# Moving PSUM banks, query buffers and the order of keys and values around a cross-attention stage, with each batch's first two heads split by rows

## The chip, the cores and the metric

The kernel runs on one core of a Trainium2 chip, in one launch. The metric is device time in microseconds (us), measured for the whole launch; the figure is the median of several runs. The engines are named as in the profile: PE (matmul), PEld (weight load, which overlaps PE), DVE (VectorE), ACT (ScalarE), POOL (GpSimd), SP (the engine that issues DMAs). Each runs its own list of instructions in order, and waits for others by semaphores.

## The reference

Four batches of 512 rows with 512 features go through four blocks, each added to the residual `x` with a gate (the tanh of a given number). Cut to what matters:

```python
# 1: selective scan over the context (512 rows x 256), gated by the normed x
x = x + tanh(g_xattn[0]) * ssm(ctx, layernorm(x), ...)        # 16 states per channel
# 2: ternary FFN: activations rounded to 8 bits, weights to -1, 0, 1
x = x + tanh(g_ffn[0]) * out(silu(gate(xn)) * val(xn))        # hidden 2048
# 3: cross attention, 16 heads of 128
q = rmsnorm((xn @ Wq).reshape(B, Sq, H, D), gq)
k = rmsnorm((ctx @ Wk).reshape(B, Skv, H, D), gk)
v = (ctx @ Wv).reshape(B, Skv, H, D)
attn = softmax(einsum('bqhd,bkhd->bhqk', q, k) * scale)
x = x + tanh(g_xattn[1]) * (einsum('bhqk,bkhd->bqhd', attn, v).reshape(B, Sq, H * D) @ Wo)
# 4: four experts, row r goes to expert r % 4
x = x + tanh(g_ffn[1]) * (silu(gate) * up) @ down
```

## The kernel before

**Work and its stages.** Products in fp16 are made of high and low halves: `split` (L238) writes both halves of a tile from PSUM or SBUF, the high half on ACT (L240), the low half on DVE (L241), and `mm3` (L243) makes three matmuls per pair (L249). The stages, per batch b:

- `front(b)` (L487) prepares the scan's inputs from context and x; `scan(b)` (L569) runs the recurrence, with most of its work on DVE (L622) and POOL (L183), and exps on ACT (L615).
- `bitnet(b)` (L670) is the ternary FFN. It ends with four updates of x, one per block of 128 rows (L755).
- `attention(b)` (L779) returns generators that the main loop steps through: `keys` (L799, per group of four heads: pk, ksq, kT), `values` (L850), `queries` (L865: weights wq by DMA, twelve matmuls into pq, high and low half qT, the squares sq), `query_norms` (L882: psq, ssq, and rqs on POOL), `scores` (L898: ps, and its row maxima nmx on DVE), `softmax` (L907: exps pr on ACT, normed high and low halves hl, and a transposing DMA to pT), `weight` (L952: pav), `weighted_sum` (L961: oT), `project` (L966, per four heads: pwo, added to x). `prepare(t)` norms one block of 128 rows and transposes it into axnT.
- `early_experts` (L1098) runs the experts of batches 0 to 2, `last_experts` (L1124) those of batch 3, behind its attention.

**The prologue** (L1162 to L1223) uses pools that close at its end: `pro` in SBUF and `psp`, four PSUM banks. It runs front and scan of batch 0; makes the ternary weights (`ternary`, tiles w8 with the tag "v", of VB buffers, stored to DRAM); runs the ternary FFN of batch 0, with `prepare` behind each row block; then `first_values` (L338), which computes batch 0's values from all four groups' weights, into tiles ov (tag "v" as well, VB buffers), and stores them in DRAM; then the weights of the attention's first groups, the keys of group 0, and the contexts of batches 2 and 3. When these pools have closed, `psa` opens (L1224): four PSUM banks, two with the tag "m" for pq, pk, pw, psq, pav and pwo, two with the tag "s" for ps. With it opens `at` in SBUF (L1226), which holds v, wq, qT, pr, hl, pT, oT and wo. Another four PSUM banks, `pss`, exist from the outset and serve front, scan, the ternary FFN and the experts. `ak` is an SBUF pool that exists from the outset, with axnT, sq, the keys and their weights.

**The main loop** (L1256 to L1297) runs over units i = (batch, head). At unit i it takes the query phase of unit i+2, the score phase of i+1 and the weighting phase of i, interleaved in ten slots. Between the slots it feeds the scan and FFN of the next batch: `rate` grows by RATE_S (0.5) or RATE_B (0.8) per slot, and a step is taken for each whole; LEADS says how many units ahead of a batch its scan begins. At the slots KPOS (5 and 9) a piece of the next group's keys is made. Other work, the staging of weights and the early experts, is filled in behind softmax's exps.

A scheduler (Tile) adds the semaphores to this order; each engine runs its own part of the program in order. When a tile takes a buffer or bank, it waits until the last use of the one before is over.

Of the kernel before, what the change touches and what calls it, by code (L numbers as in the profile page):

```python
# [30 lines left out]
F16 = mybir.dt.float16  # L31
# [9 lines left out]
P = 128  # L41
B = 4
L = 512
# [49 lines left out]
PT = 3  # L93
MT = 0
AV = 4
VB = 2
WB = 5
ATAG = {"ps": "s"}
ABUF = {"m": 2, "s": 2}
LO_POOL = {(b, h, 1) for b in range(3) for h in range(9, 16)}  # L100
HL = 2
PRE = 1
LEADS = {1: 16, 2: 17, 3: 17}
SZR = 12
NEXT = 2
LEAD_B = 6

# [2 lines left out]
def flamingo_kernel(  # L110
# [20 lines left out]
    def psum(pool, name, tag="m", bufs=None):  # L131
        if tag == "a":
            role = name.rstrip("_0123456789")
            tag = ATAG.get(role, "m")
            bufs = ABUF[tag]
        kw = {} if bufs is None else {"bufs": bufs}
        return pool.tile([P, 512], F32, tag=tag, name=name, **kw)
# [100 lines left out]
    def split(w, hi, lo, S):  # L238

        nc.scalar.activation(hi, w, AF.Copy, scale=S)  # L240
        nc.vector.scalar_tensor_tensor(lo, w, S, hi, ALU.mult, ALU.subtract)  # L241
# [537 lines left out]
    def attention(b):  # L779
# [13 lines left out]
                "q" if b else "t",  # L793
            )

        kns, vals, kqs, probs = [None] * NG, [None] * NG, [None] * NH, [None] * NH
        scs, nmxs = [None] * T, [None] * 2

        def keys(hg, ps_tile=ap):  # L799
# [62 lines left out]
                nc.sync.dma_start(wv.rearrange("p s k c -> p (s k c)"), wv_d[hg])  # L862
                vals[hg] = list(values_of(b, hg, wv, ap, v_tile))

        def queries(i):  # L865
            hg, h = divmod(i, HG)
            hn = f"{b}{hg}{h}"
            wq = at.tile([P, 2, T, HD], F16, tag="wq", name=f"wq{hn}", bufs=WQ)
            nc.sync.dma_start(wq.rearrange("p s k c -> p (s k c)"), wq_d[hg][:, h * 1024 : (h + 1) * 1024])

            ps = ap(f"pq{hn}")
            xnT = xnTs[0]
            mm3(ps, [(wq[:, 0, k], wq[:, 1, k], xnT[:, 0, k], xnT[:, 1, k]) for k in range(T)])
            sq = ak.tile([P, L], F32, tag="sq", name=f"sq{hn}", bufs=2)
            qT = at.tile([P, 2, L], F16, tag="qT", name=f"qT{hn}", bufs=2)
            split(ps, qT[:, 0], qT[:, 1], gqs)
            nc.scalar.activation(sq, ps, AF.Square, scale=QS)
            kqs[i] = [kns[hg][h // 2][:, :, :, h % 2], qT, sq]  # L880

        def query_norms(i):  # L882
            hg, h = divmod(i, HG)
            hn = f"{b}{hg}{h}"
            sq = kqs[i][2]
            ps = ap(f"psq{hn}")
            for c in range(T):
                nc.tensor.matmul(  # L888
                    ps[:, c : c + 1], sq[:, c * P : (c + 1) * P], ones[:, 0:1],
                    start=True, stop=True,  # L890
                )
            ssq = sm(T, "ssq", f"ssq{hn}")
            nc.scalar.activation(ssq, ps[:, 0:T], AF.Identity, bias=ceq[hg], scale=gfac)  # L893
            rqs = sm(T, "rqs", f"rqs{hn}")
            rsqrt(rqs, ssq)
            kqs[i][2] = rqs

        def scores(i, c):  # L898
            kT, qT, _ = kqs[i]
            rows = slice(c * P, (c + 1) * P)  # L900
            ps = ap(f"ps{b}{i}_{c}")
            mm3(ps, [(qT[:, 0, rows], qT[:, 1, rows], kT[:, :, 0], kT[:, :, 1])])
            nmx = nmxs[i % 2]
            nc.vector.tensor_reduce(nmx[:, c : c + 1], ps, AX.X, ALU.max, negate=True)  # L904
            scs[c] = ps

        def softmax(i, c0):  # L907

            rqs = kqs[i][2]
            hn = f"{b}{i}_{c0}"  # L910
            two = slice(c0, c0 + 2)
            nmx = nmxs[i % 2]
# [34 lines left out]
            nc.sync.dma_start_transpose(  # L947
                pT.rearrange("p c s k r -> p (c s k) r"), hl.rearrange("p c s k -> p (c s k)")
            )
            probs[i].append(pT)  # L950

        def weight(i, half, ps):  # L952
            hg, h = divmod(i, HG)
            cols = slice(h * HD, (h + 1) * HD)
            pT = probs[i][half]
            mm3(
                ps[:, half * 256 : (half + 1) * 256],
                [(v[:, 0, cols], v[:, 1, cols], pT[:, :, 0, k], pT[:, :, 1, k]) for k, v in enumerate(vals[hg])],
            )

        def weighted_sum(i, ps):  # L961
            o = at.tile([P, 2, L], F16, tag="oT", name=f"oT{b}{i}", bufs=4)
            split(ps, o[:, 0], o[:, 1], 1.0 / PS)
            return o

        def project(hg, os):  # L966
            nm = f"{b}{hg}"
# [12 lines left out]
                xr = xt[:, t, :]  # L980
                nc.vector.scalar_tensor_tensor(xr, ps, fo, xr, ALU.mult, ALU.add)

        os = []

        def step(i, phase):

            hg, h = divmod(i, HG)
            if phase == 0:  # L990
                if h == 0:
                    if i == 0 and b > 0:
                        for t in range(T):
                            prepare(t)
                    if KL == 0 and kns[hg] is None:
                        run(keys(hg))
                    if b < PRE:
                        values(hg)
                yield
                queries(i)  # L1000
                yield
                query_norms(i)
            elif phase == 1:
                probs[i] = []
                nmxs[i % 2] = sm(T, "nmx", f"nmx{b}{i}")
                scores(i, 0)
                yield
                scores(i, 1)
                softmax(i, 0)
                yield  # L1010
                scores(i, 2)
                yield
                scores(i, 3)
                softmax(i, 2)
            else:
                if h == 0 and b >= PRE:
                    values(hg)
                ps = ap(f"pav{b}{i}")
                for half in range(2):
                    weight(i, half, ps)  # L1020
                    yield
                os.append(weighted_sum(i, ps))
                if h == HG - 1:
                    project(hg, os)
                    os.clear()

        return step, keys, prepare

# [130 lines left out]
                    fill.pop(0)  # L1159

    ak = ctx.enter_context(tc.tile_pool(name="ak", bufs=1))
    with tc.tile_pool(name="pro", bufs=1) as pro, tc.tile_pool(name="psp", bufs=4, space=PSUM) as psp:  # L1162

        psv = pss

# [7 lines left out]
            wider["t"] = pro, MT  # L1173

        def iter_ps(name):
            return psum(psp, name, "mn"[int(name[-1]) % 2], 2)

        w3 = [
            ternary(pro, psv, [gate_wT[k * P : (k + 1) * P, :] for k in range(4)], [P, HID], 0, True),
# [24 lines left out]
        for name, bias in (("gate", gate_b), ("val", val_b)):  # L1204
# [4 lines left out]
        steps[0] = step  # L1209

        run(bitnet(
            0, wide, lambda name: psum(psp, name, "n", 2), biases, prepare, lambda name: psum(psp, name, "m", 2)
        ))


        def aside(name):
            return psum(pss, name)

        run(first_values(pro, aside))
        run(attention_weights(range(EARLY), pss))  # L1220
        run(keys(0, aside))
        for b in range(2, B):
            context(b, bigt, junk, psv, bigt)  # L1223
    psa = ctx.enter_context(tc.tile_pool(name="psa", bufs=4, space=PSUM))  # L1224
    at_pool = ctx.enter_context(ExitStack())
    at = at_pool.enter_context(tc.tile_pool(name="at", bufs=1))  # L1226

# [6 lines left out]
            estats[b][t] = row_stats(x_sb[b][:, t, :], f"e{b}{t}", XS, const.tile([P, 2], F32, name=f"est{b}{t}"))  # L1234

    in_bitnet = [False]
    behind, rate = [], 0.0

    def layer0(b):

# [11 lines left out]
            yield  # L1252


    n = B * NH
    for i in range(-2, n):  # L1256
        b2, h2 = divmod(i + 2, NH)
        for b4, lead in LEADS.items():
            if i + 2 + lead == b4 * NH:
                behind.append((b4, layer0(b4)))  # L1260
        while behind and behind[0][0] <= b2:
            run(behind.pop(0)[1])
        if KL == 0 and h2 == 0 and 0 < b2 < B:
            atts[b2] = attention(b2)
        if h2 == 0 and 0 < b2 < B:
            steps[b2] = atts[b2][0]
        if h2 == 0 and 0 < b2 < B:
            steps[b2] = atts[b2][0]
        q = steps[b2](h2, 0) if i + 2 < n else iter(())
        s = steps[(i + 1) // NH]((i + 1) % NH, 1) if 0 <= i + 1 < n else iter(())  # L1270
        w = steps[i // NH](i % NH, 2) if i >= 0 else iter(())
        for k, g in enumerate((q, s, q, s, w, s, w, s, w, q)):
            next(g, None)
            if behind:
                rate += RATE_B if in_bitnet[0] else RATE_S
                while rate >= 1 and behind:
                    rate -= 1
                    if next(behind[0][1], behind) is behind:
                        behind.pop(0)
            if k in KPOS:  # L1280
                j, c = divmod((i + 2) * len(KPOS) + KPOS.index(k) - KOFF, 4 * len(KPOS))
                j += 1
                b3, hg3 = divmod(j, NG)
                if c < 4 and 0 < j and b3 < B:
                    if c == 0 and hg3 == 0:
                        atts[b3] = attention(b3)
                    if c == 0:
                        keygen = atts[b3][1](hg3)
                    next(keygen)
                    if c == 3:  # L1290
                        next(keygen, None)
        if i == -2:
            fill.append(attention_weights(range(EARLY, NG), None))
        if i >= 0 and i % NH == NH - 1:
            finish(i // NH)
        if i == n - NH + STAGE_E:
            fill.append(early_experts())  # L1297
    while fill:
        filler(mark[0])
# [70 lines left out]
```

## Time and profile before

| what | us |
|---|---|
| runs shown | 2036.04, 2039.12, 2039.02 |
| median | 2039.02 |
| profiled execution | 2044.35 |
| its span | 2042.6 |
| mean granted TensorE clock | 0.874 |
| value tiles ov, first and last ACT instruction begin | 201.8 to 254.7 |
| last x update of the ternary FFN, batch 0 | 302.2 |
| first softmax exp | 338.4 |
| first scan of batch 1 | 367.7 |
| first softmax exp of batches 1, 2, 3 | 800.5, 1237.1, 1598.5 |
| last row block added by the attention of batch 3 | 2003.6 |

The table is one profiled execution but for the first two rows. The last row is followed by experts to the end of the span. A unit of attention takes some 23 to 29 us: 16 of them lie between the first exps of two batches. The profile's chain of work that ended last puts 19% of the span to PE, 7% to DVE, 5% to ACT, 5% to DMA; the rest of the page is read further down, where its lines are used. In a group's line, the form is out<-in with the program's names, then the count, the time, and what ended the idle time before it.

### The profile page before, as it was taken

The page shows a single profiled execution, that of the slowest core. Times are in us where ns is not written, and L with a number is a line of the kernel's source. Part 1 is how long each engine was busy: PE and PEld are TensorE (multiplying, and loading weights), DVE is VectorE, ACT ScalarE, POOL GpSimd, SP SyncE. Part 2 cuts the span into 40 slices and gives each one's busy share as a digit, 9 for nine tenths or more (in the row PEclk, how much of TensorE's full clock was granted, in tenths as well). Part 3 has the DMA queues.
Part 4 walks back from the last instruction along what each step waited for, and adds up shares of the span by engine and source line. Part 5 has one row for each costly group of instructions (what it writes and reads, how often), then busy time and mean ns, then how long its engine had stood idle before and what let it go on. Part 6 is the DMA issues. An engine that isn't in the chain of part 4 may idle for free. (4 is left out here: it accounts for less than half of the span.)

```text
span 2042.6 us, 27081 instructions
## 1 busy us (share of the span) xinstructions
PE 1608.2 (79%) x8238; PEld 903.3 (44%) x8238; DVE 1575.8 (77%) x2857; ACT 1320.4 (65%) x3118; POOL 1001.7 (49%) x926
## 2 busy tenths in 40 slices
PE   4465867667789877787989778778898879798988
PEld 1343322444444344454444444454444445445446
DVE  5898985999989787999887876999874555465654
ACT  5796566765758595565568663756476576757653
POOL 1884332876745378575436582765354240313211
PEclk8555987767899987899998988999999989899989
DMA  7554468789796877777658777688765775757854
GB/s 272 176 183 163 157 162 229 186 221 259 191 277 160 209 187 174 211 168 183 122 147 207 179 167 195 154 193 196 164 130 119 172 170 162 188 147 182 211 118 139
DMA packets 528242, 369.09 MB, mean 181 GB/s; under 512 B 425248, under 2 KB 427424, under 8 KB 521696
## 3 DMA queue, kind: packets, MB, share of 16 engines
q1 hardware_dynamic: 528096, 367.37, 71.0%
q8 instruction: 64, 1.05, 0.2%
q14 instruction: 82, 0.67, 0.1%
HBM read 220.22 MB, written 44.30 MB: 130 GB/s over the span
## 5 line engine op out<-in xcount | busy, mean ns | idle before, releaser
L183 POOL TENSOR_TENSOR h<-u,bc 128x512 f32<-128x512 f32 x256 | 339.3, 1346 | 84.6 <-PE py L590 49.1
L590 PE MATMUL py<-ident,h 128*128 128x128 f32 x1024 | 199.1, 339 | 135.9 <-DVE h L623 110.4
L615 ACT ACTIVATE dA<-delta,A 128x512 f32<-128x512 f32 x256 | 172.2, 685 | 137.0 <-DVE h L623 110.2
L622 DVE TENSOR_TENSOR_SCAN dA<-dA,h 128x512 f32<-128x512 f32 x200 | 240.8, 1217 | 20.1 <-POOL h L183 15.5
L249 PE MATMUL pav<-pT,v 128*128 128x256 f16 x1536 | 210.7, 294 | 47.9 <-DMA pT<-hl 19.9
L590 PEld LDWEIGHTS py<-ident,h 128*128 128x128 f32 x1024 | 164.1, 213 | 180.8 <-DVE h L623 133.8
L249 PE MATMUL ps<-kT,qT 128*128 128x512 f16 x768 | 212.5, 397 | 37.6 <-ACT pr L924 34.4
L249 PE MATMUL pq<-axnT,wq 128*128 128x512 f16 x768 | 204.9, 423 | 36.2 <-DMA axnT<-xsa 11.2
L904 DVE TENSOR_REDUCE nmx<-ps 128x1 f32<-128x512 f32 x256 | 173.2, 680 | 73.1 <-PE ps L249 72.2
L945 DVE SCALAR_TENSOR_TENSOR hl<-pr,den,hl 128x512 f16<-128x512 f32 x214 | 191.4, 911 | 30.1 <-ACT hl L942 16.7
L924 ACT ACTIVATE pr<-ps,nmx,rqs 128x512 f32<-128x512 f32 x256 | 197.1, 772 | 17.6 <-DVE hl L945 13.8
L249 PEld LDWEIGHTS <-v 128*128 128x128 f16 x1536 | 160.3, 105 | 105.9 <-issue 50.4
L249 PE MATMUL pwo<-wo,oT 128*128 128x512 f16 x768 | 180.3, 386 | 6.4 <-DVE oT L241 3.1
L944 POOL TENSOR_SCALAR hl<-pr,den 128x512 f16<-128x512 f32 x86 | 61.8, 719 | 186.9 <-issue 82.8
L249 PEld LDWEIGHTS <-wq 128*128 128x128 f16 x768 | 82.6, 109 | 147.1 <-issue 68.3
L249 PEld LDWEIGHTS <-cT 128*128 128x128 f16 x768 | 80.7, 106 | 146.0 <-issue 75.8
L183 POOL TENSOR_TENSOR g<-g,gv 128x512 f32<-128x512 f32 x64 | 84.3, 1319 | 111.1 <-DVE gv L724 56.1
L180 POOL TENSOR_TENSOR rqs<-ssq,mhalf 128x4 f32<-128x4 f32 x64 | 68.6, 1072 | 138.9 <-ACT ssq L893 123.5
L623 DVE TENSOR_TENSOR h<-dA,cc 128x512 f32<-128x512 f32 x200 | 133.8, 678 | 2.6
L249 PEld LDWEIGHTS <-qT 128*128 128x128 f16 x768 | 78.2, 103 | 122.9 <-issue 57.2
L249 PE MATMUL pk<-wk,cT 128*128 128x512 f16 x384 | 109.9, 431 | 28.2 <-ACT ssq L893 14.3
L942 ACT ACTIVATE hl<-pr,den 128x512 f16<-128x512 f32 x128 | 92.1, 719 | 54.2 <-DVE den L931 46.5
(373 smaller groups left out, 3519.4 us busy)
## 6 DMA issues: line engine op xcount, KB each, us to landing
bc<-bd SPq DMA_DIRECT2D x112, 256.0 KB, 4.3
cc<-bd SPq DMA_DIRECT2D x112, 256.0 KB, 4.2
wq<-dwq SPq DMA_DIRECT2D x64, 256.0 KB, 4.0
wo<-dwo SPq DMA_DIRECT2D x64, 256.0 KB, 4.3
w<-w3d SPq DMA_DIRECT2D x12, 1024.0 KB, 7.3
g<-in_gate_b SPq DMA_DIRECT2D x48, 256.0 KB, 4.1
gv<-in_val_b SPq DMA_DIRECT2D x48, 256.0 KB, 4.4
de<-hle SPq DMA_DIRECT2D x9, 1024.0 KB, 6.8
```

The lines of the kernel that those rows point to most:

```text
L180: nc.gpsimd.tensor_tensor(res, arg, mhalf[:, : arg.shape[1]], ALU.pow)
L183: nc.gpsimd.tensor_tensor(out, a, b, ALU.mult)
L249: nc.tensor.matmul(ps, l, r, start=first and i == 0, stop=last and i == n - 1)
L590: nc.tensor.matmul(ys[g // gs][:, g % gs, t, :], src[:, g::T], ident, is_transpose=True, start=first and t == 0 and g % gs == 0, stop=last ...
L615: last = nc.scalar.activation(dA, delta[t0 + t], AF.Exp, scale=A[:, t0 + t, n : n + 1])
L622: nc.vector.tensor_tensor_scan(dA, dA, h, 0.0, ALU.mult, ALU.add)
L623: nc.vector.tensor_tensor(h, dA, cc, ALU.mult)
L904: nc.vector.tensor_reduce(nmx[:, c : c + 1], ps, AX.X, ALU.max, negate=True)
L924: mark[0] = nc.scalar.activation(pr, scs[c], AF.Exp, bias=nmx[:, one], scale=rqs[:, one], accum_out=den[:, c - c0 : c - c0 + 1],).ins
L942: nc.scalar.activation(hl[:, c, 0], prs[c], AF.Copy, scale=den[:, one])
L944: nc.gpsimd.tensor_scalar(hl[:, c, 0], prs[c], den[:, one], 1.0, ALU.mult, ALU.mult)
L945: nc.vector.scalar_tensor_tensor(hl[:, c, 1], prs[c], den[:, one], hl[:, c, 0], ALU.mult, ALU.subtract)
```

## The change

- `psa` is opened ahead of the prologue and stays; `psp` is gone, and the prologue takes its banks from psa's two tags.
- wq and qT move from `at` to `ak`, and so exist from the outset. They take 8 KB a partition there; in the prologue VB goes from 2 to 1, so w8 and ov have one buffer each time.
- In the prologue, the attention's first weights and the keys of group 0 come ahead of `first_values`.
- Units: the first SPLIT = 2 heads of each batch go by halves of the rows: head 0 with rows 0 and 1 (blocks of 128), head 1 with the same, then head 0 with rows 2 and 3, head 1 with those. Each half has its own wq load, pq, psq, pav and their evictions. For half units `rate` grows half as fast, and keys are made at one slot instead of two; LEADS counts halves as halves.
- In batch 3, the tiles pk, pw and psq come from `pss`, which the scan no longer uses then.

The diff, cut to its core:

```diff
-VB = 2
+VB = 1
+LAST_PSS = ("pk", "pw", "psq")
+SPLIT = 2
...
             role = name.rstrip("_0123456789")
+            if pool is psa and role in LAST_PSS and name[len(role)] == str(B - 1):
+                return psum(pss, name)
...
-        def queries(i):
+        def queries(i, cs):
...
-            hn = f"{b}{hg}{h}"
-            wq = at.tile([P, 2, T, HD], F16, tag="wq", name=f"wq{hn}", bufs=WQ)
+            hn = f"{b}{hg}{h}_{cs[0]}"
+            cols = slice(cs[0] * P, (cs[-1] + 1) * P)
+            wq = ak.tile([P, 2, T, HD], F16, tag="wq", name=f"wq{hn}", bufs=WQ)
...
-            mm3(ps, [(wq[:, 0, k], wq[:, 1, k], xnT[:, 0, k], xnT[:, 1, k]) for k in range(T)])
+            mm3(ps[:, cols], [(wq[:, 0, k], wq[:, 1, k], xnT[:, 0, k, cols], xnT[:, 1, k, cols]) for k in range(T)])
...
-            qT = at.tile([P, 2, L], F16, tag="qT", name=f"qT{hn}", bufs=2)
-            split(ps, qT[:, 0], qT[:, 1], gqs)
-            nc.scalar.activation(sq, ps, AF.Square, scale=QS)
+            qT = ak.tile([P, 2, L], F16, tag="qT", name=f"qT{hn}", bufs=2)
+            split(ps[:, cols], qT[:, 0, cols], qT[:, 1, cols], gqs)
+            nc.scalar.activation(sq[:, cols], ps[:, cols], AF.Square, scale=QS)
...
-        def weighted_sum(i, ps):
-            o = at.tile([P, 2, L], F16, tag="oT", name=f"oT{b}{i}", bufs=4)
-            split(ps, o[:, 0], o[:, 1], 1.0 / PS)
-            return o
+        def weighted_sum(i, ps, cs):
+            cols = slice(cs[0] * P, (cs[-1] + 1) * P)
+            if i not in oTs:
+                oTs[i] = at.tile([P, 2, L], F16, tag="oT", name=f"oT{b}{i}", bufs=4)
+            split(ps[:, cols], oTs[i][:, 0, cols], oTs[i][:, 1, cols], 1.0 / PS)
...
-    with tc.tile_pool(name="pro", bufs=1) as pro, tc.tile_pool(name="psp", bufs=4, space=PSUM) as psp:
+    psa = ctx.enter_context(tc.tile_pool(name="psa", bufs=4, space=PSUM))
+    with tc.tile_pool(name="pro", bufs=1) as pro:
...
-        run(first_values(pro, aside))
         run(attention_weights(range(EARLY), pss))
         run(keys(0, aside))
+        run(first_values(pro, aside))
         for b in range(2, B):
             context(b, bigt, junk, psv, bigt)
-    psa = ctx.enter_context(tc.tile_pool(name="psa", bufs=4, space=PSUM))
...
+    ab = (tuple(range(T)), (0, 1), (2, 3))
+    units = []
+    for b in range(B):
+        units += [(b, h, ab[1 + half]) for h0 in range(0, SPLIT, 2) for half in range(2) for h in (h0, h0 + 1)]
+        units += [(b, h, ab[0]) for h in range(SPLIT, NH)]
+    n = len(units)
...
-                rate += RATE_B if in_bitnet[0] else RATE_S
+                rate += (RATE_B if in_bitnet[0] else RATE_S) * (1 if whole_unit else 0.5)
...
-            if k in KPOS:
+            if k in KPOS[0 if whole_unit else 1 :]:
```

The other lines of the diff carry the rows `cs` of a unit through the phases; the early experts are appended at the same head of batch 3 as before.

## The prediction

> **What bounds the kernel now.** I read the page's shares first, then the windows by stage, and only then the stretches that the change touches: PE's timeline at the start of each batch's attention, the value tiles of the prologue, and what PE waits for in batch 3.
>
> The page's span and busy shares:
>
> ```profile
> span 2042.6 us, 27081 instructions
> ...
> PE 1608.2 (79%) x8238; PEld 903.3 (44%) x8238; DVE 1575.8 (77%) x2857; ACT 1320.4 (65%) x3118; POOL 1001.7 (49%) x926
> ```
>
> No engine is the bound over the whole span; that has to be read by stage. The windows have, after the stretch's limits and length, the busy time of PE, PEld, DVE, ACT and POOL, the granted clock, the DMA share and GB/s:
>
> ```profile
> 190.00:302.00 112.00, 83.64 (x325) 34.70 (x324) 95.81 (x249) 61.20 (x124) 42.58 (x41) 0.84 0.54 155
> 302.00:366.00 64.00, 42.61 (x137) 17.79 (x138) 38.50 (x78) 44.09 (x105) 18.84 (x23) 0.73 0.81 230
> 366.00:590.00 224.00, 158.40 (x805) 101.51 (x805) 216.32 (x354) 149.49 (x378) 157.76 (x132) 0.79 0.85 222
> ...
> 1596.00:1994.00 398.00, 342.37 (x1817) 188.26 (x1817) 220.69 (x440) 260.23 (x674) 92.80 (x102) 0.93 0.70 169
> ```
>
> Three things are in them. From 366 to 590 (batch 0's attention beside batch 1's scan) DVE is busy 216.32 of 224 us, 97%: it is the bound there. In the 64 us just before, between the end of the first ternary FFN (its last update of x is at 302.2) and the first scan of batch 1 (367.7), DVE is idle 25.5 us: a hole ahead of a stage that DVE bounds, so whatever DVE does in the hole comes off the stage. And from 1596 (batch 3's attention, no scan beside it) PE is busy 342.37 of 398: PE bounds, with 56 us of waits.
>
> PE's timeline at the hole and at the three changes of batch (start, length, line, tile, count, and in brackets the idle time before):
>
> ```profile
> 326.01 5.28 PE L249 MATMUL pq<-axnT,wq 128*128 128x512 f16 x12 [5.74 <-DMA wq<-dwq]
> 333.07 1.47 PE L249 MATMUL ps<-kT,qT 128*128 128x512 f16 x6
> ...
> 783.39 5.30 PE L249 MATMUL pq<-axnT,wq 128*128 128x512 f16 x12 [11.25 <-DMA axnT<-xsa]
> ...
> 795.14 2.75 PE L249 MATMUL pq<-axnT,wq 128*128 128x512 f16 x12
> ...
> 1208.43 4.44 PE L249 MATMUL pq<-axnT,wq 128*128 128x512 f16 x12 [4.56 <-issue]
> ...
> 1584.96 5.28 PE L249 MATMUL pq<-axnT,wq 128*128 128x512 f16 x12 [2.53 <-issue]
> ```
>
> The first queries at 326.01 wait for their weights: the tile lives in a pool that opens only when the prologue's pools have closed, so SP issues the load at 319.95. At 783 PE waits 11.25 us for all four transposed row blocks, and the twelve matmuls after a pause take 5.30 instead of 2.75 us.
>
> **Part 1: the start of batch 0.** Keys come ahead of the values, and psa, wq and qT exist from the outset. By the changed order of the instructions the first two half units' queries stand on PE before the last row block of the ternary FFN, the first scores around it. Only the softmax output still waits for the late pool, and that opens when the last value tile has been stored. Added up by rows of this trace, DVE has 10.2 us more work behind it at the first scan of batch 1 than now (342.1 for 331.9 us). DVE bounds the stage behind, so up to that comes off. Nothing can come off beyond the idle time of the hole, 25.5 us, and nothing comes off if DVE is held up as long elsewhere. **Term: -9**, bounds 0 and -25; I go by the row of moved work, which is the nearer.
>
> **Part 2: one buffer in place of two (VB).** Value tiles now:
>
> ```profile
> L240 ACT ACTIVATE ov<-pw x16: 576/593/597, 201.8 to 254.7; 128x512 f16<-128x512 f32 x16
> ...
> L354 SPq DMA_DIRECT2D vd<-ov x16: 319/320/532, 203.2 to 258.6; - x16
> ...
> DMA to landing us min/median/max: 2.1/2.3/3.1
> ```
>
> With one buffer each tile must be written (ACT 0.59, then DVE 0.68), issued (0.32) and landed (2.3) before the next begins: 3.9 us, times 16 is 62 us, against some 57 today (201.8 to 258.6). They start behind the keys, by the order about where PE is at 232, and so end at 294 at best, or at 328 if each takes 6 us. Both lie ahead of the first softmax of today (338.4), so the late pool need not open later than now. What is queued behind a waiting ov is ACT's work for the ternary FFN, and DVE, busy 95.81 of 112 us in that stretch, waits for that. Earlier the twelve Signs of the ternary weights share the tag: 1.99 us each on ACT, with a store that lands in 4.6 us (median). The first four, from 66 us on, have a single dA (0.67) between them, so up to three stalls of 3.9 us, 11.7 in all; DVE is idle 7 us there anyway, waiting for POOL. The other eight have about 4.8 us of other ACT work between them and cost nothing; without that cover they would cost as much each. **Term: +4**, bounds 0 and +12.
>
> **Part 3: changes of batch.** A half unit's queries need two row blocks, not four. At batch 1 the order has only the first two blocks' transposes ahead of them; the matmuls in front are the same. To be had: the wait 11.25 and the slow matmuls 5.30 - 2.75 = 2.55, together 13.8. The transposed blocks are issued at 755.9, 769.7 (two) and 779.4, so the second is there some 10 us before the last, but PE's fillers come to an end at the same place; I take half, **-7**, bounds 0 and -13.8. At batch 2: 4.56 and 4.44 - 2.75 make 6.25, I take **-4**; at batch 3: 2.53 and 2.53, 5.06, I take **-3**; both with nothing as the other end, since the profile names no releaser there.
>
> **Part 4: batch 3's keys, values and norms in the scan's banks.** PE's waits from 1596 to 1996 (total, times, longest):
>
> ```profile
> PE pav L249 <- DVE v L241: 6.5, 4, 3.0
> PE pk L249 <- ACT ssq L893: 6.1, 3, 3.9
> PE pk L249 <- DMA wk<-dwk: 5.0, 3, 3.2
> ...
> PE pav L249 <- ACT nmx L916: 4.2, 1, 4.2
> PE psq L888 <- DVE oT L241: 3.8, 2, 2.4
> ...
> PE pw L249 <- DVE v L241: 3.0, 2, 2.1
> PE pav L249 <- DVE ksq L833: 2.7, 1, 2.7
> ```
>
> A pk that waits for ssq, a psq for oT, a pw for v, a pav for ksq wait for a bank, not for data: 6.1 + 3.8 + 3.0 + 2.7, and 1.4 of smaller ones, make 17.0. With pk, pw and psq in the four banks that the scan has left, these go. What is late next is data: ACT (260.23 of 398 busy) and the transposes, so I take half, **-8**. The other end: the experts fill the same four banks, and the order has them about one unit later than now; one new wait as long as the longest of these rows, +4. Bounds -17 and +4.
>
> **Part 5: what halves cost.** Eight extra half passes (two a batch), each with ACT's qT, sq, ssq and oT, DVE's two low parts, POOL's rqs (1.07 us), and a load of 256 KB (4.0 us to landing) on SP's queue. The columns on PE are the same: pav's 256-column matmuls show twelve in 1.3 to 1.5 us where twelve of 512 take 2.75. Fixed cost of an ACT instruction from PSUM: 128x512 takes 0.591 (sq), 128x128 0.273 (ksq); a line through both gives 0.167 fixed. 32 of them are 5.3 us over four batches; 16 more on DVE at 0.08 (from 0.68 for 512 and 1.28 for 1024 columns) 1.3 us. Of the four batches only batch 0's DVE share and batch 3's ACT share lie near a bound, **+2**, bounds 0 and +6.6. The rate of the scan between is halved for half units, so its place beside the units stays.
>
> [...]
>
> **Sum.** -9 + 4 - 7 - 4 - 3 - 8 + 2 = -25. The profiled execution took 2044.35 (span 2042.6 and 1.75 around it), which gives 2019.3. The median of the runs shown is 2039.02, 5.3 below the profiled one; on that scale I predict **2014.0**.
>
> **Rivals.**
> - *The hole is filled whole* (0.10): -20 at the start, -18 at the changes of batch, -13 in batch 3, +2: -49, **1990**. For it: DVE's 97% behind the hole. Against: softmax still waits for the last value store.
> - *The start gives nothing* (0.18): ov's waits give back on ACT what the early queries gain, and batch 3's freed banks show the softmax chain; 4 + 0 - 14 - 4 + 2 = -12, **2027**. For it: DMA is busy 0.81 and 0.85 in 302 to 590, so early loads may only come late.
> - *It does not do what it says* (0.08): every wait that is taken away is found again at the next instruction, and VB's cost eats the rest, **2039**. For it: idle stretches on PE are short, none in batch 3 over 4.2 us at a time.
> - *The single buffer decides* (0.14), slower: ACT stops for each ov's store, 2.3 us sixteen times, 37 us, with the ternary FFN's evictions queued behind it and DVE starved; 37 + 4 - 14 - 8 + 2 = +21, **2060**. It decides from the point where the stops add over 20 us to the end of the ternary FFN, that is over 1.3 us per tile, or the last store lands after some 360 us.
>
> **How the numbers follow.** The forecast has 0.50, its own range 2004 to 2025. Range **1996 to 2046**: 0.06 of the first rival lies below it, 0.11 of the last above. A measurement of this kernel can tell about 0.2% (4 us) from no change: faster 0.10 + 0.50 + 0.18 = 0.78, same 0.08, slower 0.14.
>
> **What would show it.** Right: the first softmax exp at 320 to 335 us instead of 338.4, the first scan of batch 1 earlier than 367.7; DVE idle in the 64 us before that under 18; the pq at batch 1 with under 6 us of idle before it; bank waits in batch 3 under 9 us and its 398 us some 8 shorter. Wrong: idle on ACT before ov over 20 us, the ternary FFN's last update of x after 310, the first exp after 345; or new waits of expert matmuls for pk and pw evictions in batch 3.

## The result: 0.7% slower, and where the profile shows it

The changed kernel takes 2054.23 us (median of 4 runs, 2051.05 to 2057.95) where the kernel before takes 2037.53 beside it; the ratio is 1.0072, 95% interval 1.0044 to 1.0099. The forecast was 2014, in a range of 1996 to 2046. The profiled execution took 2054.29.

The page of the changed kernel, span and busy shares:

```profile
span 2052.3 us, 27308 instructions
...
PE 1607.0 (78%) x8334; PEld 916.6 (45%) x8334; DVE 1587.2 (77%) x2873; ACT 1331.3 (65%) x3150; POOL 1003.7 (49%) x934
```

DVE and ACT each have 11 us more work; PE has the same (with a clock of 0.867 for 0.874).

PE's timeline at the first queries of each batch (for batch 2 the first two half units):

```profile
297.34 1.51 PE L253 MATMUL pq<-axnT,wq 128*128 128x256 f16 x12
...
782.93 2.74 PE L253 MATMUL pq<-axnT,wq 128*128 128x256 f16 x12 [2.26 <-DMA axnT<-xsa]
...
1217.89 2.02 PE L253 MATMUL pq<-axnT,wq 128*128 128x256 f16 x12
...
1231.02 2.27 PE L253 MATMUL pq<-axnT,wq 128*128 128x256 f16 x12
...
1602.90 2.36 PE L253 MATMUL pq<-axnT,wq 128*128 128x256 f16 x12
```

PE stood idle 11.25, 4.56 and 2.53 us ahead of the first queries of batches 1, 2 and 3 before; now 2.26 us and nothing that the view shows. The waits are all but gone, but the queries come half a us earlier at batch 1, and later at the others: at 782.93, 1217.89 and 1602.90 for 783.39, 1208.43 and 1584.96. Nor do the halves alone take the long wait away: in the profile of the changed kernel with whole units (the first of the experiments) the first queries of batches 1 and 2 show no more than this:

```profile
785.64 4.71 PE L253 MATMUL pq<-axnT,wq 128*128 128x512 f16 x12 [2.47 <-DMA axnT<-xsa]
...
1211.50 2.75 PE L253 MATMUL pq<-axnT,wq 128*128 128x512 f16 x12 [2.25 <-DMA axnT<-xsa]
```

And the kernel is slower, so time must be lost elsewhere. Marks that mean the same in both kernels find it (us from the start; the first four heads of a batch are 16 exps, whether they go by halves or not):

| mark | before | changed | difference |
|---|---|---|---|
| ternary FFN of batch 0 ends | 302.2 | 315.3 | +13.0 |
| first softmax exp | 338.4 | 327.8 | -10.6 |
| first scan of batch 1 | 367.7 | 383.8 | +16.0 |
| first exp of batch 1 | 800.5 | 796.9 | -3.6 |
| first exp of head 4, batch 1 | 904.4 | 923.0 | +18.5 |
| first exp of batch 2 | 1237.1 | 1235.3 | -1.8 |
| first exp of head 4, batch 2 | 1330.8 | 1355.2 | +24.5 |
| first exp of batch 3 | 1598.5 | 1614.9 | +16.5 |
| last row block added by attention | 2003.6 | 2013.3 | +9.7 |

Up to the first exp of batch 2 nothing is lost against the kernel before. The first four heads of batches 1 and 2, in which the halves lie, take 22 and 26 us longer; batch 1 makes it good, batch 2 gives back 8 us. From head 4 of batch 3 to the end of the span the changed kernel is 9 us quicker.

The value tiles of the changed kernel (ranges are the starts of the first and the last):

```profile
L244 ACT ACTIVATE ov<-pw x16: 572/597/597, 243.7 to 322.3; 128x512 f16<-128x512 f32 x16
...
L358 SPq DMA_DIRECT2D vd<-ov x16: 319/328/531, 245.3 to 323.7; - x16
its engine sat idle before it (us, times) until:
  DMA vd<-ov: 17.0, 9
```

With one buffer ACT stood 17.0 us behind the stores of these tiles (3.3 before), and 5.6 us more at the ternary weights. But the FFN's lateness does not grow with these waits: its four row blocks end at 260.7, 275.6, 301.4 and 315.3, for 248.0, 263.3, 288.3 and 302.2 before. It is 12.7 us late at the first of them, when ACT had stood 2.8 us behind an ov's store, and 13.0 at the last. Ahead of the first block lie the attention's first weights and keys, some 24 us of ACT's work that came later before.

PE's waits in batch 3, from 1613 to 2013:

```profile
PE pav L253 <- DMA pT<-hl: 14.5, 6, 4.6
PE ps L253 <- ACT pr L931: 7.3, 8, 3.3
PE pk L253 <- DMA wk<-dwk: 7.1, 2, 6.3
PE ps L253 <- DMA kT<-ks: 4.1, 1, 4.1
```

None of the waits that were counted as waits for a bank, 17.0 us (psq for oT, pk for ssq, pw for v and the smaller ones), is left; of that kind only a pq shows, 1.1 us behind a sq. What comes up in their place is data: transposes of pT, weights, and the exps.

### The profile page after: what moved, and what is told of

Same layout as the page of the kernel before. It is cut to its first block, busy times and chain, and to the rows that moved or that the text cites. A ratio compares the mean times of both kernels' runs of the same rounds, so it can differ in the third digit from the quotient of the medians.

```text
span 2052.3 us, 27308 instructions
## 1 busy us (share of the span) xinstructions
PE 1607.0 (78%) x8334; PEld 916.6 (45%) x8334; DVE 1587.2 (77%) x2873; ACT 1331.3 (65%) x3150; POOL 1003.7 (49%) x934
## 5 line engine op out<-in xcount | busy, mean ns | idle before, releaser
L187 POOL TENSOR_TENSOR h<-u,bc 128x512 f32<-128x512 f32 x256 | 334.7, 1325 | 79.3 <-PE py L594 44.0
L253 PE MATMUL pav<-pT,v 128*128 128x256 f16 x1536 | 217.2, 297 | 64.8 <-DMA pT<-hl 44.7
L594 PEld LDWEIGHTS py<-ident,h 128*128 128x128 f32 x1024 | 168.4, 213 | 165.8 <-DVE h L627 118.9
L253 PE MATMUL pq<-axnT,wq 128*128 128x512 f16 (+1 forms) x864 | 207.2, 396 | 23.4 <-ACT ssq L900 6.5
L952 DVE SCALAR_TENSOR_TENSOR hl<-pr,den,hl 128x512 f16<-128x512 f32 x214 | 200.1, 953 | 32.4 <-ACT hl L949 18.2
L951 POOL TENSOR_SCALAR hl<-pr,den 128x512 f16<-128x512 f32 x86 | 66.0, 767 | 211.4 <-issue 100.9
L253 PEld LDWEIGHTS <-wq 128*128 128x128 f16 x864 | 94.3, 110 | 122.6 <-issue 49.9
L184 POOL TENSOR_TENSOR rqs<-ssq,mhalf 128x4 f32<-128x4 f32 (+1 forms) x72 | 72.0, 1000 | 129.6 <-ACT ssq L900 126.7
```

The costliest lines, as they stand in the source:

```text
L184: nc.gpsimd.tensor_tensor(res, arg, mhalf[:, : arg.shape[1]], ALU.pow)
L187: nc.gpsimd.tensor_tensor(out, a, b, ALU.mult)
L253: nc.tensor.matmul(ps, l, r, start=first and i == 0, stop=last and i == n - 1)
L594: nc.tensor.matmul(ys[g // gs][:, g % gs, t, :], src[:, g::T], ident, is_transpose=True, start=first and t == 0 and g % gs == 0, stop=last ...
L951: nc.gpsimd.tensor_scalar(hl[:, c, 0], prs[c], den[:, one], 1.0, ALU.mult, ALU.mult)
L952: nc.vector.scalar_tensor_tensor(hl[:, c, 1], prs[c], den[:, one], hl[:, c, 0], ALU.mult, ALU.subtract)
```

## The experiments

Each was timed beside the kernel before; the ratios carry the comparison, since that kernel's own median was between 2037 and 2041. Single executions of one kernel spread by up to some 10 us either way, so a profile alone tells no more than that.

**Parts undone or alone.** Whole units in the changed kernel:

```diff
-SPLIT = 2
+SPLIT = 0
```

> The change without the halves (whole units from the start), all else as changed. In the profile of the changed kernel the attention of batch 2 ends 30 us later against its start than before (1252.5 to 1640.2, where it was 1260.1 to 1618.3), and the ternary FFN of batch 0 ends 13 us later. Theory H (the halves reorder attention against scan and FFN, and batch 2 loses by it): the 30 us of batch 2 go, the gains of 4 to 8 us at two changes of batch go too, so 2054 - 30 + 15 = some 2039, batch 2's attention within 5 us of 358. Rival P (the prologue's serial tiles and order make the loss, and batch 2 slips for another reason, such as batch 3's keys in the scan's banks): no less than 2050, batch 2 still 380 or more.

Measured: 2024.99, ratio 0.9927 (0.9898 to 0.9955). Without the halves the rest of the change is 0.7% faster than before: the halves cost 29 us, nearly twice what the change loses. The time is below theory H's 2039, and batch 2's attention took 369 us, not the 358 that theory H had. Against this kernel the changed one is 6 us ahead at the first exp of batch 1 and 6, 23 and 30 behind at those of batches 2 and 3 and at the end of the span. The whole-unit kernel is the fastest of the versions here, with its like at other rates further down.

```diff
-LAST_PSS = ("pk", "pw", "psq")
+LAST_PSS = ()
```

> The change with batch 3's keys, values and norms back in attention's own banks. Group 0 of batch 3's keys is made in batch 2's last units, so this also takes them out of the banks of the FFN. Theory H: batch 3's attention gives back the 12 us that it gained against before (22 late at its start, 10 at its end), so 2064 to 2068, batch 2 unchanged at some 388. Rival L (the scan's banks are contended at the end of batch 2): batch 2 gets 10 us or more shorter, so 2045 to 2055 in all.

Measured: 2067.02, ratio 1.0139 (1.0099 to 1.0180). The banks are worth some 13 us in the changed kernel, as theory H said, and rival L (contention at the end of batch 2) is out: batch 2's stage did not get shorter.

The old order of the prologue (values, then weights and keys), all else as changed:

> The change with the old order in the prologue: the values ahead of the weights and keys. Theory P (a single buffer is what costs in the prologue): the value tiles lie in the FFN again with one buffer each time, the FFN of batch 0 ends as late as in the changed kernel (315) or later, total 2052 to 2062. Rival O (the keys and weights ahead are what makes the FFN late): the FFN ends near 302 to 306, and the total is 2042 to 2048.

Measured: 2058.40, ratio 1.0093 (1.0063 to 1.0123). The FFN ended 20 us later than before, not 13, so with one buffer the new order is no cost. Its cause of lateness is another, though: in the old order the value tiles stand in the FFN and ACT waits for their stores there; in the new order the weights and keys stand there.

Halves alone, on the kernel before:

> The kernel before with the halves alone: two buffers, old pools, old order, no foreign banks. Theory H: the halves alone cost batch 2 its 30 us and give 8 to 15 at the changes of batch: 2055 to 2062. Rival P: they are harmless, 2028 to 2040.

Measured: 2058.43, ratio 1.0088 (1.0063 to 1.0114). The halves cost 18 us without any other part of the change. The kernel with halves, the new prologue and the old banks (2067.02) differs from it in the prologue alone, and is 9 us slower (the intervals of the two ratios just overlap): with halves the new prologue is no gain.

The banks alone, on the kernel before:

> The kernel before with batch 3's keys, values and norms in the scan's banks, and nothing else. The changed kernel without this lost 13 us (2067 for 2054). Theory K (the banks are a gain of their own, whatever else is changed): 2039 - 13, so 2022 to 2030. Rival: the banks pay only behind the other changes: 2034 to 2042.

Measured: 2033.82, ratio 0.9968 (0.9951 to 0.9984): 6 us, and neither of the two cases; a gain of their own, half the size that they have behind the rest.

The new prologue alone (SPLIT 0, LAST_PSS empty):

> The new prologue alone: early banks and buffers, keys ahead of values, one buffer; whole units, old banks in batch 3. Theory K (the banks make all the gain of the whole-unit version, the prologue neither gains nor loses): 2033 to 2042. Rival V (the single buffer and the late FFN, 14 us at its end, stay lost): 2045 to 2053.

Measured: 2028.64, ratio 0.9946 (0.9917 to 0.9975). Better than either case: it gains 11 us though its FFN ends 13 us later. The same kernel with halves is the run with 2067.02: here the halves cost 38 us, more than in the changed kernel (29) or alone (18). So their price depends on what else is changed, and the prologue that was made for them gains only without them. Its profile (20 us shorter than the profile before, where the medians differ by 10) has the gain behind the first exp of batch 1 (1.5 us earlier than before) and ahead of that of batch 2 (12.4), in the order of the work; which part of it brings that, no run tells.

One buffer alone, on the kernel before:

```diff
-VB = 2
+VB = 1
```

> The kernel before with one buffer for the tiles w8 and ov, and nothing else. Theory of the forecast (the store of each tile is mostly hidden): +4, 2038 to 2048, the FFN of batch 0 ends within 8 us of 302. Rival V (the single buffer makes the FFN's 13 us by itself, through ACT standing behind the stores): the FFN ends at 312 or later, 2048 to 2056.

Measured: 2051.46, ratio 1.0056 (1.0038 to 1.0075). Its value tiles:

```profile
L240 ACT ACTIVATE ov<-pw x16: 573/597/598, 203.4 to 282.8; 128x512 f16<-128x512 f32 x16
...
  DMA vd<-ov: 20.9, 12
```

ACT stood 20.9 us behind the stores. The FFN's row blocks came 6.5, 12.5, 14.9 and 15.2 us later, one after the other, and the first exp 10.8 later: rival V, for the old order, in which the value tiles lie in the FFN. There the buffer that paid for the early banks costs 11 us; the new prologue gains despite it.

**Which batches, and why.** Halves in some batches alone:

```diff
-        units += [(b, h, ab[1 + half]) for h0 in range(0, SPLIT, 2) ...
...
+        split_b = SPLIT if b in (0,) else 0
+        units += [(b, h, ab[1 + half]) for h0 in range(0, split_b, 2) ...
```

> The change with halves in batch 0 alone; whole units in batches 1, 2 and 3. From the profiles with and without halves, measured from the end of one batch's attention to the end of the next: the halves gain 14 us up to the end of batch 0's attention, lose 21 in batch 1, 18 in batch 2, 5 in batch 3. Theory H says these are separate prices: 2025 (whole units everywhere) - 14 = some 2011. Rival S (batch 0's gain is only a loan, taken back by batch 1 whatever its units are): 2022 to 2030.

Measured: 2035.90, ratio 0.9983 (0.9959 to 1.0006). The expected gain of 14 us is a loss of 11, above even rival S's 2030.

> Halves in batches 0 and 3. Theory H: 5 us later than with batch 0 alone, so some 2016. If batch 3's halves help at the change of batch, where no scan runs beside: 2005 to 2010.

Measured: 2047.90, ratio 1.0030 (1.0014 to 1.0046). Batch 3's halves cost some 10 to 12 us (by the ratios and by the medians), where no scan runs beside. PE's waits in the first four heads of batch 3, with whole units (82 us, from 1601) and then with halves (97 us, from 1604):

```profile
PE ps L253 <- ACT pr L931: 3.4, 1, 3.4
PE ps L253 <- DMA kT<-ks: 3.3, 1, 3.3
PE pav L253 <- DMA pT<-hl: 3.0, 2, 2.6
```

```profile
PE pq L253 <- DMA wq<-dwq: 7.7, 2, 7.1
PE pav L253 <- DMA pT<-hl: 6.0, 3, 3.4
PE ps L253 <- ACT pr L931: 3.3, 2, 3.1
PE peg0a L253 <- DMA exT<-xse: 2.2, 1, 2.2
```

The longer waits are those for a unit's weights and transposes. That a half unit has fewer matmuls to cover them is a reading of these two profiles; no run shows it by itself.

> The changed kernel with halves in batches 1 and 2 alone, whole units in 0 and 3. If the prices add up: 2025 + 6 = 2031. By the stages of the profiles (first four heads 20 and 18 us later, some of it given back): 2037 to 2050.

Measured: 2049.65, ratio 1.0050 (1.0028 to 1.0072): 25 us above whole units, as the stages had it. The prices do not add up: 11 for batch 0, 12 for batch 3 behind it, 25 for batches 1 and 2, and 29 for all. From the first exp of a batch to that of its head 4, in us, each from one profile:

| kernel | batch 1 | batch 2 | batch 3 | time |
|---|---|---|---|---|
| before (whole) | 104 | 94 | 88 | 2039 |
| whole units | 103 | 94 | 82 | 2025 |
| halves in batch 0 | 106 | 109 | 82 | 2036 |
| halves in 0 and 3 | 107 | 107 | 97 | 2048 |
| halves in 1 and 2 | 121 | 116 | 82 | 2050 |
| changed (all) | 126 | 120 | 90 | 2054 |

Batch 2 took 109 and 107 us with whole units of its own where batch 0 had halves, and 103 with whole units at the rate of 0.49 further down, so a part lies in the order that the scheduler makes of the whole. What the first four heads lose comes back in part: from head 4 to the next batch's first exp the changed kernel takes 312 us in batch 1 and 260 in batch 2, with whole units 323 and 269.

The first four heads of batch 2, whole units and then the changed kernel (windows; busy PE, PEld, DVE, ACT, POOL, then clock, DMA share and GB/s):

```profile
1229.00:1323.00 94.00, 76.66 (x399) 45.23 (x397) 81.30 (x140) 58.55 (x155) 52.10 (x50) 0.89 0.73 168
```

```profile
1235.00:1355.00 120.00, 89.74 (x485) 54.93 (x486) 99.87 (x158) 65.81 (x170) 70.03 (x64) 0.89 0.72 170
```

DVE is busy 86% and 83%, and in the second 18.6 us more DVE work lies in the stage. 9 more scans stand ahead of head 4 there (counted in the trace); their instructions make 15.6 us of it, and the same 16 low parts hl 4.6 more. So the scan runs ahead of the attention there; whether that is what the halves cost, two experiments asked.

The scan fed half as fast in half units of batches 1 to 3:

```diff
-                rate += (RATE_B if in_bitnet[0] else RATE_S) * (1 if whole_unit else 0.5)
+                rate += (RATE_B if in_bitnet[0] else RATE_S) * (1 if whole_unit else 0.25 if b2 else 0.5)
```

> The changed kernel, with the scan and FFN of the next batch fed half as fast again during the half units of batches 1 to 3 (0.25 in place of 0.5). At the first row maxima of head 4 in batches 1 and 2, DVE has 10 and 12 scans more behind it in the changed kernel than before. Theory A (the scan runs ahead of the attention there, and the attention is left alone at the batch's end): the surplus goes, and with it 15 to 30 of the 39 us that halves lose in batches 1 and 2: 2025 to 2040. Rival C (the chain through a half unit is too short for its latencies, whatever the scan does): 2050 to 2060.

Measured: 2036.59, ratio 0.9982 (0.9961 to 1.0004): 18 us of the loss came back. But the surplus that theory A names did not go: 183 and 248 scans stood ahead of the two marks, for 184 and 250. The size is A's, its mechanism is not shown.

```diff
-LEADS = {1: 16, 2: 17, 3: 17}
+LEADS = {1: 16, 2: 17, 3: 16}
```

> The changed kernel with the scan and FFN of batch 3 begun one unit later (16 units ahead of its attention in place of 17). Theory A (with halves they are used up early in batch 2, and DVE is idle 100 us in batch 2 where it is 84 with whole units): 5 to 15 us gained, 2039 to 2049. Rival C (the loss is in the half units themselves): 2050 or more.

Measured: 2057.73, ratio 1.0073 (1.0048 to 1.0098). Nothing gained: rival C. A later start doesn't move the scan out of those heads (250 ahead of the mark again), so theory A falls as far as the start is concerned.

The second load of the weights taken away:

```diff
-            wq = ak.tile([P, 2, T, HD], F16, tag="wq", name=f"wq{hn}", bufs=WQ)
-            nc.sync.dma_start(wq...
+            if cs[0] == 0:
+                wqs[i] = ak.tile([P, 2, T, HD], F16, tag="wq", name=f"wq{hn}", bufs=WQ)
+                nc.sync.dma_start(wqs[i]...
+            wq = wqs[i]
```

> The changed kernel, but a head's second half keeps the query weights of its first (no second load of 256 KB; eight loads fewer). Rival W (the second loads make the halves' cost: the queries of batch 3 waited up to 7.1 us for wq): 10 us or more gained, 2044 or less. Theory A (the order): 2050 to 2057.

Measured: 2049.98, ratio 1.0051 (1.0029 to 1.0073), against the changed kernel's 1.0072 (1.0044 to 1.0099): 4 us by the medians, within both intervals. Rival W is out as the main cause.

**The added instructions, and how far order alone goes.** Whole units, but with the first two heads' matmuls and evictions cut in two:

> Whole units everywhere, in the order without halves, but in each batch's first two heads the query matmuls, the qT halves, sq, ssq, rqs and oT run as two instructions of half the size: all that the halves add, but for the second load of wq. Theory H/A/C (order and waits, not instructions): 2025 to 2030, near the kernel with whole units. Rival I (the fixed costs of the added instructions): the larger part of the 29 us comes back, 2040 or more.

Measured: 2049.22, ratio 1.0044 (1.0021 to 1.0066): 24 us above whole units, rival I by its size. And with the query matmuls alone cut in two:

> Whole units everywhere; in each batch's first two heads only the query matmuls run as two sets of twelve on 256 columns, with 96 more matmuls and weight loads in all and nothing added on ACT, DVE or POOL. In the traces a pair of half sets takes 1.47 + 1.47 us for 2.75, so the work is 8 x 0.2 = 1.6 us more. Theory H with the added work as its cause: 2025 to 2032. Rival Z: 2036 or more, as with all evictions halved (2049), since the order moves as much.

Measured: 2038.45, ratio 0.9998 (0.9980 to 1.0016): 13 us for 1.6 us of work. A cause cannot be its own work alone, then. In both, the order moves as well: the longest sequence that DVE keeps in common with the whole-unit kernel has 2108 and 2074 of 2857 instructions (by operation and tile). Was it that?

```diff
-RATE_S = 0.5
+RATE_S = 0.49
```

> The changed kernel with whole units, with RATE_S 0.49 in place of 0.5: the scan beside attention is fed 2% slower. Nothing is added or removed; the scheduler's order moves in places. This measures how far the order alone moves the time. Theory H (the halves cost some 29 us of their own): within 6 us of the whole-unit kernel's 2025. Rival Z (the scheduler's order is so sensitive that a difference of 20 us between two versions needs no cause in their work): 10 us or more away, on either side.

Measured: 2023.03, ratio 0.9930 (0.9907 to 0.9954).

> The same with RATE_S 0.51. Theory H: 2019 to 2031. Rival Z: 10 us or more from 2025.

Measured: 2025.49, ratio 0.9939 (0.9917 to 0.9961). In both the sequence moves, if less (2316 and 2475 of 2857 instructions keep theirs), and the whole-unit kernel stays within 2 us.

> The changed kernel as it is, with halves, and RATE_S 0.51. Theory H: 2048 to 2060, near the 2054 of the changed kernel, 25 us above the kernel with whole units at the same rate. Rival Z: 2044 or less, or 2064 or more.

Measured: 2045.23, ratio 1.0040 (1.0022 to 1.0058). The kernel with halves moves 9 us by the same 2% (6.5 by the ratios, whose intervals overlap), below the expected interval and above rival Z's.

So moves of the order that leave the work alone aren't worth 29 us among whole units, though they were smaller moves than those that came with the cuts. All eleven versions that cut something in two and have the changed kernel's banks lie at 2035.9 or above. The halves' price is real, and some of it moves with the order.

Its cause stays open. The cut instructions alone make 24 us, but elsewhere: by the profiles that kernel is 15 us behind whole units at the first exp of batch 1, where the changed one is 6 ahead. The scan's place goes with neither: with the slower feed 183 and 248 scans stood ahead of the two marks and the price was 12 us, with the cut instructions 179 and 243 and it was 24. The granted clock is not it: its mean over the executions was 0.877 with whole units and 0.873 in the changed kernel, and among executions of one kernel 0.001 less went with some 0.6 us more, which makes some 2.5 of the 29 us, an estimate.

## Why the prediction was wrong, step by step

The halves carry two terms of the sum, -14 (Part 3) and +2 (Part 5), together -12; with and without them the changed kernel shows +29. That is the miss of 40 us. The other three, -9, +4 and -8, make -13, and the kernel without halves is 14 us faster; as the parts below show, that is luck for the first two of the three.

- **What bounds the kernel**: batch 3 paid for PE's waits. That DVE bounds the stage behind the hole agrees with its 97%; no run tests it alone. The reading missed that DVE is as near its bound beside the halves of batch 1. Its first four heads, before and changed (windows as above):

```profile
800.00:904.00 104.00, 83.07 (x441) 52.78 (x439) 99.25 (x154) 63.26 (x160) 71.23 (x63) 0.89 0.72 182
```

```profile
797.00:923.00 126.00, 98.66 (x530) 63.68 (x529) 120.44 (x182) 73.58 (x183) 87.25 (x79) 0.88 0.75 185
```

- **Part 1, -9 at the start**: the first exp came at 327.8, within the stated 320 to 335. DVE was busy 43.44 us in the 64 us ahead of the first scan of batch 1, for 38.50 before:

```profile
303.70:367.70 64.00, 43.04 (x138) 17.79 (x139) 38.50 (x74) 45.10 (x105) 20.37 (x23) 0.73 0.81 226
```

```profile
319.80:383.80 64.00, 44.09 (x155) 19.73 (x156) 43.44 (x83) 49.37 (x111) 17.86 (x21) 0.69 0.84 236
```

So some 5 of the 10.2 us went into the hole (idle 20.6 us, not under 18), but the hole ended 16 us later. From there to the first exp of batch 1 the changed kernel was 20 us quicker (413.1 for 432.8), which little more than paid that back. The step that failed is that the scan would start no later for it. The late FFN alone does not explain that: with whole units it ended at 316.6, and the first scan came at 369.3. The scan came at 380 to 392 in all the versions with batch 0's halves behind early banks and one buffer, and at 364.9 with the halves alone. Without halves the new prologue does gain 11 us, but behind batch 1's first exp, not here.
- **Part 2, +4 for one buffer**: mis-sized; alone it costs 11 us. The forecast's sign of being wrong, the FFN's last update after 310, came true at 315.3. The step that failed is weighing the tiles' own chain (62 us for some 57) and the opening of the late pool. In the old order the FFN stood behind the stores, with ACT idle 20.9 us for them, and ended 15 us later; in the new order it was as late by the weights and keys put ahead of the values, for which the forecast has no term. The rival that named the stores put them at +37 us and slower from 20 on; the FFN ended 13 us later, below that point, and the kernel with one buffer and whole units is faster (2025). It named the right side for another reason.
- **Part 3, -14 at the changes of batch**: the waits went as said (11.25 to 2.26, 4.56 and 2.53 to nothing), but with whole units they fell as well (2.47 and 2.25 at batches 1 and 2), so the halves are not shown to be what took them. The step that failed is counting a wait that goes as time that is won: the first exp of batch 1 came 3.6 us earlier and that of batch 2 1.8 us, and the next four heads took it back several times over.
- **Part 4, -8 for the banks**: right in mechanism, and about right in size: 6 us alone, 13 in the changed kernel, 4 between the new prologue alone and the whole-unit kernel (within their intervals). The counted bank waits are gone, and data is late next.
- **Part 5, +2 for halves**: the failing step of the whole. It priced the halves by the fixed time of their added instructions. By instructions it was too low, but not by much:

The evictions of the changed kernel, whole and half (the last column of numbers before the idle time is the mean in ns):

```profile
L245 DVE SCALAR_TENSOR_TENSOR qT<-pq,gqs,qT 128x512 f16<-128x512 f32 x56 | 41.5, 741 | 12.4 <-ACT qT L244 12.3
...
L244 ACT ACTIVATE qT<-pq,gqs 128x512 f16<-128x512 f32 x56 | 38.1, 680 | 12.8 <-PE pq L253 12.8
...
L245 DVE SCALAR_TENSOR_TENSOR qT<-pq,gqs,qT 128x256 f16<-128x256 f32 x16 | 7.7, 480 | 7.2 <-ACT qT L244 7.2
...
L244 ACT ACTIVATE qT<-pq,gqs 128x256 f16<-128x256 f32 x16 | 7.5, 468 | 10.7 <-PE pq L253 10.7
```

Two halves cost 2 x 480 - 741 = 219 ns more on DVE, where 80 was reckoned from a row out of PSUM (0.68 us for 512 columns) and one out of SBUF (1.28 for 1024), and 2 x 468 - 680 = 256 on ACT (2 x 377 - 594 = 160 for sq), where 167 was. A half pair of query matmuls takes 1.47 + 1.47 us for 2.75. With sq, with ssq and oT (359 and 169 ns more on ACT), and with oT on DVE (146 ns), eight extra halves make some 10 us over four batches on ACT and DVE, an estimate from these means, and 1.6 on PE. The price was 18, 29 or 38, by what else was changed. So the time of the added instructions is not the price: the whole-unit kernel lost 24 us by the cut instructions alone and 13 by the 1.6 us of cut matmuls. The forecast also took only batch 0's DVE and batch 3's ACT to lie near a bound, where DVE was busy 99.25 of 104 us in the first heads of batch 1. What turns 10 us of work into 18 to 38 is not shown. Chains with half the matmuls to cover them, and the new order around them, are what the profiles suggest; the first cannot be all of it, since the kernel with cut instructions has whole units.

## What to carry to other kernels

Cutting a unit so that its first piece can start early can cost several times the added instructions (here 18 to 38 us for some 10), for reasons that a sum of instructions does not show: time the cut alone, and with and without the edits that it is to go with, since its price changed with them. A wait that disappears from the profile is a gain only if the next common mark comes earlier: compare marks with the same meaning over the whole kernel, not waits. And ask of a buffer that is given up who stands behind the instruction that will wait for it, in its engine's order: in the kernel with one buffer alone the FFN's evictions stood behind 20.9 us of waits for stores that nobody needed soon.

## What the runs showed of the hardware that was not expected

The slow matmuls of 5.3 us for twelve, in the forecast put down to the pause ahead of them, need not stand right behind it, nor did a shorter wait make them quick. The windows have the granted clock third from the end: the half set at 782.93 (2.74 us, behind 2.26 us of idle time), a quick one of 1.47 us, and the set at 1231.02 (2.27 us, no idle time right ahead) with the two stretches in front of it:

```profile
782.90:785.60 2.70, 2.67 (x13) 1.92 (x14) 1.53 (x2) 1.82 (x3) 2.70 (x4) 0.50 1.03 203
791.97:793.40 1.43, 1.43 (x16) 1.30 (x14) 1.43 (x2) 0.22 (x1) 1.19 (x1) 1.00 1.17 254
1223.00:1228.50 5.50, 0.93 (x7) 0.58 (x6) 0.95 (x3) 3.11 (x10) 3.52 (x5) 0.76 1.08 238
1228.50:1231.00 2.50, 2.49 (x12) 1.72 (x12) 0.75 (x1) 1.23 (x2) 1.14 (x1) 0.50 0.51 105
1231.00:1233.30 2.30, 2.30 (x15) 1.66 (x13) 0.69 (x1) 0.60 (x1) 0.07 (x1) 0.64 0.46 93
```

The slow sets ran at a granted clock of 0.50 and 0.64, the quick one at 1.00. At 1231.02 the pause (4.31 us) lies one group of matmuls earlier, and the clock was still low behind that group. So the 2.55 us that the forecast booked beside the 11.25 us wait did not come with the shorter wait.
